# Rows gathered one by one from two issuing engines: five chunks on ScalarE, twenty on the sync engine

## The chip, the core and the metric

The kernel runs on one NeuronCore of a Trainium2 chip. The metric is the device time of one execution in microseconds. A core has a matrix engine (TensorE, PE in the profile; its weight loads are PEld), VectorE (DVE), ScalarE (ACT), GpSimd (POOL) and a sync engine (SP), each with its own queue of instructions that runs in order. DMAs are issued from the queues of SP, ACT and POOL and carried out by 16 DMA engines. Engines wait for each other through semaphores.

## The reference

```python
h = jnp.maximum(_layernorm(x, axis=-1), 0.0)          # x: (12500, 128) f32
msgs = h[src]                                         # src, dst: 200000 edges, sorted by dst
agg = jax.ops.segment_sum(msgs, dst, num_segments=12500)
deg = jax.ops.segment_sum(jnp.ones((200000,)), dst, num_segments=12500)
agg = agg / jnp.maximum(deg, 1.0)[:, None]
y = jax.nn.relu(agg @ Wg + h @ Ws + bg)               # 128 -> 128
y = jnp.tanh(y @ W1 + b1)                             # 128 -> 512
y = jnp.tanh(y @ W2 + b2)                             # 512 -> 512
return x + (y @ W3 + b3)                              # 512 -> 128
```

One layer of a graph network: each node's feature row is normalised, the rows of its neighbours are averaged, and a small network of three layers follows. The edges are sorted by destination.

## The kernel before

**Set-up.** The normalised rows h are written to a table in DRAM, `htab` (lines 221 to 239). The 200000 edges are cut into 1563 chunks of 128 edges.

**One chunk.** The 128 source rows of a chunk come into a tile of 128 x 128. DVE builds a one-hot matrix from the destinations of eight chunks at a time (`onehot`, line 364: a comparison at 372 and a column sum at 382 for the degrees), in four buffers `oh_bufs` that are used in turn. PE multiplies rows by one-hot matrix (`add`, line 422) and so adds the rows to the sums of a block of 512 nodes in PSUM. All matmuls are recorded at line 290, all transposes at line 293, all activations at line 322, all copies on ScalarE at line 325.

**Three ways for rows to arrive.**

- `gather` (line 301): an indirect DMA issued by POOL fetches the 128 rows of a chunk from `htab` with an index column. It is recorded at line 303 as `rows<-htab,scol`. 1465 chunks come so, in the order of the list `order`. The pool `rows_in` has `AHEAD` = 48 tiles, and the loop issues a gather once `nxt < behind + AHEAD`; on the chip a gather waits until PE has used the tile's former content.
- 80 chunks (`raw`) are gathered straight from x during the set-up, and normalised later.
- `row_loads` (line 327): 18 chunks, listed in `slow`, are fetched row by row by the sync engine: `place` holds the byte offsets of their rows; a register load (line 333) takes 32 of these to registers, and 32 DMAs of 512 bytes each, one row each, follow (line 341, recorded at 299). A chunk takes four such sets, 128 DMAs. The pool `rows_one` has four tiles, so that rows are loaded long before they are used.

**The list of slow chunks.** A chunk is put on the list after every `EACH` = 72 others:

```python
if n <= 0:
    slow.append(c)
    n = EACH
else:
    n -= 1
```

**The network.** When the sums of a block are complete, its layers are worked off in small parts between the chunks: `go_on` issues one part (at most a matmul or two, and the activation that follows) after every second chunk (lines 678 to 680). ScalarE's Relu, Tanh and bias additions are needed by PE's next parts. DVE scales the sums (`mT`, line 523) and adds x at the end (`o`, line 579); `ps_t` and `ps_b` have one PSUM buffer each. From chunk `QUICK` = 1376 on the parts are placed by estimated times.

**Order.** `tc.keep_in_program_order` fixes each engine's instructions in the order in which the Python loop writes them. A part of the row loads is written per step of the loop (line 655): `next(loading, 0)` issues `TOGETHER` = 4 row DMAs each time the count of gathered chunks behind the loop passes another 72 x 4 / 128 = 2.25. Also on the sync engine's queue: the own rows of a block (`hb`, line 476), x (`xb`, line 499), and the stores of the result (`sp_dma` in `store`, 12 chunks after the sum, `LATE`). DMAs of the sync engine and of ScalarE share eight semaphores, which the framework hands out in turn; a DMA that gets a semaphore waits until the DMA that had it before has landed.

Of the kernel before, what the change touches and what calls it, by code (L numbers as in the profile page):

```python
# [22 lines left out]
F32 = mybir.dt.float32  # L23
# [8 lines left out]
P = 128  # L32
# [5 lines left out]
NRAW = 10  # L38
RAW0 = 256
STEP = 40  # L40
AHEAD = 48
SLOW0 = 160
EACH = 72
TOGETHER = 4
LOADS = 32
LATE = 12
LEAD = 16
QUICK = 1376
# [11 lines left out]
def windowed(ctx, tc, x, src, dst, Wg, Ws, bg, W1, b1, W2, b2, W3, b3, out, flag):  # L60
    nc = tc.nc
    N, D = x.shape
# [18 lines left out]
    def raw(c):  # L81
        return RAW0 <= c < RAW1 and (c - RAW0) % STEP < GRP


    slow, n = [], 0
    for c in range(SLOW0, NCH - 12):
        if raw(c):
            continue
        if n <= 0:
            slow.append(c)  # L90
            n = EACH
        else:
            n -= 1


    def first(w, span=per):
# [8 lines left out]
    blocks, n = [], 0  # L105
# [10 lines left out]
    rows_one = ctx.enter_context(tc.tile_pool(name="rows_one", bufs=4))  # L116
    rows_in = ctx.enter_context(tc.tile_pool(name="rows_in", bufs=AHEAD))
    ps_c = ctx.enter_context(tc.tile_pool(name="ps_c", bufs=1, space=PSUM))
# [8 lines left out]
    for t, a in ((rsrc, src), (rdst, dst)):  # L127
        a = a[RAW0 * P : RAW1 * P].rearrange("(u e) -> u e", u=NRAW)[:, : GRP * P]
# [46 lines left out]
    def centre(pool, xt, k, stats, bufs=2):  # L175
        nc.vector.tensor_reduce(stats[:, 0], xt, AX.X, ALU.add)
        nc.vector.scalar_tensor_tensor(xt, spread(stats[:, 0], k), -1.0 / D, xt, op0=ALU.mult, op1=ALU.add)
        sq = pool.tile([P, k, D], F32, name=f"sq{k}", bufs=bufs)
        nc.scalar.activation(sq, xt, AF.Square)
        nc.vector.tensor_reduce(stats[:, 1], sq, AX.X, ALU.add)  # L180

    def factors(stats):
        nc.scalar.activation(stats[:, 1], stats[:, 1], AF.Sqrt, bias=eps, scale=1.0 / D)
        nc.vector.reciprocal(stats[:, 1], stats[:, 1])
# [4 lines left out]
    with tc.tile_pool(name="setup", bufs=1) as sp, tc.tile_pool(name="ln", bufs=2) as ln:  # L189
# [59 lines left out]
        for c0, w in WINDOWS[1:]:  # L249
            v = low[:, c0:]  # L250
# [44 lines left out]
    def flat(t):  # L295
        return t.rearrange("p a b -> p (a b)")

    def sp_dma(*a):
        tc.keep_in_program_order(nc.sync.dma_start(*a))  # L299

    def gather(c):
        r = rows_in.tile([P, D], F32, name="rows")
# [7 lines left out]
    ROWB = 4 * D  # L310
    hbytes = htab.rearrange("n d -> (n d)").bitcast(U8)
# [3 lines left out]
    place = const.tile([len(slow), P], I32, name="place")  # L315
# [8 lines left out]
        def copy(*a):  # L324
            tc.keep_in_program_order(nc.scalar.copy(*a))

    def row_loads():
        for i, c in enumerate(slow):
            r = rows_one.tile([P, D], F32, name="srows")
            rows_t[c] = r  # L330
            rb = r.bitcast(U8)
            for p0 in range(0, P, LOADS):
                loads, vs = nc.values_load_multi_w_load_instructions(
                    place[i : i + 1, p0 : p0 + LOADS], engines=[mybir.EngineType.SP], min_val=0,
                    max_val=(N - 1) * ROWB,
                    skip_runtime_bounds_check_because="src holds rows of x, as the indirect DMAs take it to",
                )
                for ld in loads:
                    tc.keep_in_program_order(ld)
                for p, v in enumerate(vs, p0):  # L340
                    sp_dma(rb[p : p + 1, :], hbytes[bass.ds(v, ROWB)].rearrange("(o b) -> o b", o=1))
                    if (p + 1) % TOGETHER == 0:
                        yield

    def raw_stats(i):
        return stats_raw[:, :, i * GRP : (i + 1) * GRP]

    def raw_scaled(i):
        h = raw_rows[i]
        scale(h, h, GRP, raw_stats(i))  # L350
        for j in range(GRP):
            rows_t[RAW0 + i * STEP + j] = h[:, j]
# [11 lines left out]
    def onehot(g):  # L364
        k = min(GRP, NCH - g * GRP)
        lo, w = window(g * GRP)
        is_raw = raw(g * GRP)
        oh = ed.tile([P, GRP, W_RAW], F32, name="ohr", bufs=2) if is_raw else oh_bufs[g % OHS]
        if not is_raw and w < oh_w[g % OHS]:
            nc.vector.memset(oh[:, :, w : oh_w[g % OHS]], 0.0)  # L370
            oh_w[g % OHS] = w
        nc.vector.tensor_tensor(  # L372
            oh[:, :k, :w], lane[:, None, :w].to_broadcast([P, k, w]),
            dloc[:, g * GRP : g * GRP + k][:, :, None].to_broadcast([P, k, w]), op=ALU.is_equal,
        )
        ohs[g] = oh
        step, n = (oh.shape[2], w) if is_raw else (PITCH - per, w + per * (k - 1))
        cnt = ed.tile([P, PITCH], BF16, name="cnt", bufs=16)
        part, row, col = oh.ap
        shifted = bass.AP(tensor=oh.tensor, offset=oh.offset, ap=[part, [col[0], n], [step * col[0], k]])  # L380
        with nc.allow_low_precision(reason="whole numbers up to the chunks of a group"):
            nc.vector.tensor_reduce(cnt[:, :n], shifted, AX.X, ALU.add)  # L382
        counts[g] = (lo, n, cnt)
# [10 lines left out]
    def count(b):  # L394

        n, m = blocks[b]
        dg = flat(ps_m.tile([P, 4, P], F32, name="pm"))
        groups = sorted({c // GRP for c in reach[b]})
        for g in groups:
            lo, w, cnt = counts[g]  # L400
            a0, a1 = max(lo, n), min(lo + w, n + m)
            pe.matmul(
                dg[:, a0 - n : a1 - n], ones, cnt[:, a0 - lo : a1 - lo], start=(g == groups[0]), stop=(g == groups[-1]),
                skip_group_check=True,
            )
        rd = ml.tile([P, BLK], F32, name="rd", bufs=3)
        nc.vector.tensor_scalar(rd[:, :m], dg[:, :m], 1.0, None, op0=ALU.max)  # L407
        nc.vector.tensor_reduce(total[:, b : b + 1], dg[:1, :m], AX.X, ALU.add)
        nc.vector.reciprocal(rd[:, :m], rd[:, :m])  # L409
        rds[b] = rd  # L410
# [189 lines left out]
        )  # L600

    order = [c for c in range(NCH) if not raw(c) and c not in slow]
    loading = row_loads()
    work, done, nxt, behind = [], 0, 0, 0
    ngrp = -(-NCH // GRP)
    span = BLK // per
# [2 lines left out]
    def store(upto):  # L609
        while stores and stores[0][0] <= upto:  # L610
            sp_dma(*stores.pop(0)[1:])

    def soonest():
        two = work[: 2 if len(work) > 1 and work[1][3] < work[0][3] and work[0][4] else 1]
        return min(two, key=lambda w: max(w[2], now), default=None)
# [16 lines left out]
    for c in range(NCH):  # L632
        g = c // GRP
        at = c
        store(c if c >= QUICK else c - LATE)
        if c % GRP == 0 and g + 2 < ngrp:
            onehot(g + 2)
            if raw((g + 2) * GRP):
                raw_scaled(((g + 2) * GRP - RAW0) // STEP)
            if 2 <= g < 2 + NRAW:  # L640
                centre(ed, raw_rows[g - 2], GRP, raw_stats(g - 2), bufs=1)
            if g == 2 + NRAW:
                factors(stats_raw)

        while c % GRP == GRP // 2 and counted < len(blocks) and reach[counted][-1] // GRP <= g + (c >= QUICK):
            count(counted)
            counted += 1
        while nxt < len(order) and nxt < behind + AHEAD:
            gather(order[nxt])
            nxt += 1  # L650
        if not raw(c) and c not in slow:
            behind += 1
            batch = behind * P // (EACH * TOGETHER)
            if behind > SLOW0 - 3 * EACH and batch > (behind - 1) * P // (EACH * TOGETHER):
                next(loading, 0)
        if c >= QUICK:

            there = 7.5 + 1.251 * (NRAW * GRP + order.index(c)) if c not in slow else 0
            while soonest() and max(now, soonest()[2]) < there:
                go_on(soonest())  # L660
            now = max(now, there) + 0.27
        add(c)

        lead = LEAD if c < QUICK else 2
        if done < len(blocks) and (c - lead if across[done] else c) >= reach[done][-1]:
            if across[done]:
                merge(done)
            quick = reach[done][-1] + LEAD >= QUICK

            before = done - 1 if done and reach[done - 1][-1] + LEAD < QUICK else None  # L670
            work.append([layers(done, before), 0, 0, 0, quick and blocks[done][1] <= P])
            done += 1

        if c % span == span - 10 and (c // span + 1) * BLK < N:
            own_turned(c // span + 1)
            if (c // span + 2) * BLK < N:
                own(c // span + 2)
        if c < QUICK:
            if c % 2 == 0:
                go_on(work[0] if work else None)  # L680
        if c == QUICK:
            for b, (_, n) in enumerate(blocks):
                if n < BLK:
                    own_part(b)
# [379 lines left out]
```

## Time and profile before

| | |
|---|---|
| median of 11 runs | 2327.13 us (2317.41 to 2333.45) |
| the profiled execution | 2333.16 us, its span 2331.2 us |
| granted TensorE clock, mean | 0.791 |
| PE busy | 1322.9 us (57%) |
| DVE busy | 1066.6 us (46%) |
| POOL busy | 1463.3 us (63%) |
| ACT busy | 227.2 us (10%) |
| gathers from `htab` on POOL | 1465, 945 ns each |
| one-row DMAs on the sync engine | 2304, from 117 to 2070 us |

The profile is of one execution. Busy time counts instructions that compute or, on POOL, make the descriptors of a gather; DMA-issuing instructions on SP and ACT do not count as busy (they stand under SPq and ACTq). "Idle before" is the time in which an engine stood still just before an instruction, followed by what ended it as far as the semaphores tell; "remote" is a releaser that the profile could not name, "issue" a wait for nothing that it shows. The set-up takes the first 110 us; POOL's first gather from `htab` starts at 111 us and the last ends at 2268 us.

### The profile page before, as it was taken

To read this page: it belongs to the slowest core of one execution; us is meant where nothing else is said; L and a number is where in the kernel's file an instruction comes from. 1 tells how busy PE (TensorE), PEld (TensorE's weight loads), DVE (VectorE), ACT (ScalarE), POOL (GpSimd) and SP (SyncE) were. 2 spreads that over 40 slices of the span, in tenths; PEclk is the share of its full clock that TensorE was granted. 3 is DMA by queue.
4 is the path that set the end of the run, shared out by engine and by line. 5 is a ranking of instruction groups with operands and counts; after the bars stand their busy time and mean duration, and the time that the engine had idled before them with its cause. 6 is when DMAs were issued, how large, how long until landed. Compare 5 with 4: busy or idle time off the path is not lost. (4 is left out here: it accounts for less than half of the span.)

```text
span 2331.2 us, 19720 instructions
## 1 busy us (share of the span) xinstructions
PE 1322.9 (57%) x5212; PEld 866.5 (37%) x5212; DVE 1066.6 (46%) x651; ACT 227.2 (10%) x362; POOL 1463.3 (63%) x1553
## 2 busy tenths in 40 slices
PE   0132345556766766765565665565655655654668
PEld 0022233334444444443343433343433433432437
DVE  5924283545446544643443453443534434533522
ACT  1100010001111011101000000000000000010013
POOL 7675656666666656666666666666666666646650
PEclk9998567788887877877787787777877887776879
DMA  6721111212222212212222222222222221221210
GB/s 166 217 53 39 51 46 51 55 51 60 61 54 56 59 51 55 60 51 55 52 61 55 51 60 55 52 57 55 54 58 55 55 55 51 60 54 45 64 46 9
DMA packets 124131, 139.34 MB, mean 60 GB/s; under 512 B 32776, under 2 KB 98454, under 8 KB 123816
## 3 DMA queue, kind: packets, MB, share of 16 engines
q0 software_dynamic: 49440, 101.35, 17.1%
q1 hardware_dynamic: 71374, 33.32, 5.2%
q10 hardware_dynamic: 3196, 3.32, 0.6%
q8 instruction: 43, 0.70, 0.1%
q14 instruction: 78, 0.64, 0.1%
HBM read 125.06 MB, written 12.82 MB: 59 GB/s over the span
## 5 line engine op out<-in xcount | busy, mean ns | idle before, releaser
L303 POOL DMA_INDIRECT rows<-htab,scol x1465 | 1384.8, 945 | 778.3 <-issue 338.9
L290 PE MATMUL pm<-h,w 128*128 128x512 f32 (+4 forms) x1344 | 716.1, 628 | 185.1 <-ACT h L322 113.3
L372 DVE TENSOR_TENSOR oh<-shared,dloc 128x1152 f32<-128x1152 f32 (+2 forms) x186 | 243.8, 1316 | 914.3 <-remote 370.6
L290 PEld LDWEIGHTS agg<-oh,rows 128*128 128x128 f32 x2098 | 387.5, 225 | 468.2 <-issue 418.2
L290 PE MATMUL agg<-oh,rows 128*128 128x144 f32 (+3 forms) x2098 | 435.1, 329 | 221.0 <-issue 179.7
L382 DVE TENSOR_REDUCE cnt<-oh 128x200 bf16<-128x1600 f32 (+2 forms) x186 | 525.0, 2827 | 4.8
L290 PEld LDWEIGHTS pm<-h,w 128*128 128x128 f32 x1344 | 242.6, 220 | 225.8 <-ACT h L322 122.3
L290 PEld LDWEIGHTS edge<-oh,rows 128*128 128x128 f32 x832 | 149.9, 216 | 145.9 <-issue 140.9
L290 PE MATMUL edge<-oh,rows 128*128 128x144 f32 (+2 forms) x832 | 160.4, 312 | 37.2 <-issue 34.5
L293 PE MATMUL pt<-ident,hb 128*128 128x128 f32 x98 | 26.1, 410 | 233.8 <-DVE o L579 184.4
L322 ACT ACTIVATE h<-pm,b2c 128x512 f32<-128x512 f32 (+4 forms) x112 | 70.9, 633 | 665.7 <-remote 244.9
L290 PE MATMUL pm<-mT,wg 128*128 128x512 f32 (+4 forms) x56 | 42.3, 848 | 122.2 <-DVE mT L523 106.7
L293 PEld LDWEIGHTS pt<-ident,hb 128*128 128x128 f32 x98 | 16.5, 206 | 241.3 <-DVE o L579 189.5
L322 ACT ACTIVATE h<-pm,b1c 128x512 f32<-128x512 f32 (+4 forms) x112 | 69.1, 632 | 265.9 <-remote 183.2
L146 POOL DMA_INDIRECT raw<-in_x_dram,rsrc x80 | 77.6, 970 | 25.6 <-issue 24.1
L290 PE MATMUL pm<-cnt,ones 128*128 128x200 bf16 (+7 forms) x294 | 38.7, 233 | 84.0 <-issue 83.8
L409 DVE RECIPROCAL rd<-rd 128x512 f32<-128x512 f32 (+4 forms) x28 | 81.8, 2920 | 0.0
L407 DVE TENSOR_SCALAR rd<-pm 128x512 f32<-128x512 f32 (+4 forms) x28 | 17.3, 620 | 115.7 <-remote 75.4
L290 PEld LDWEIGHTS <-ones 128*128 128x128 bf16 x294 | 23.8, 101 | 95.5 <-issue 94.8
L290 PEld LDWEIGHTS pm<-mT,wg 128*128 128x128 f32 x56 | 11.4, 254 | 127.2 <-DVE mT L523 110.8
L322 ACT ACTIVATE h<-pm,bgc 128x512 f32<-128x512 f32 (+4 forms) x28 | 17.7, 632 | 356.4 <-PE agg L290 159.1
L205 PE MATMUL pm<-ident,idx_f 98*128 98x98 f32 x32 | 6.2, 376 | 75.8 <-issue 75.8
(68 smaller groups left out, 496.4 us busy)
## 6 DMA issues: line engine op xcount, KB each, us to landing
srows<-htab SPq DMA_DIRECT2D x2304, 0.5 KB
rows<-htab,scol POOLq DMA_INDIRECT x1465
hb<-htab SPq DMA_DIRECT2D x24, 256.0 KB
xb<-in_x_dram SPq DMA_DIRECT2D x23, 256.0 KB
out_dram<-o SPq DMA_DIRECT2D x23, 256.0 KB
htab<-h SPq DMA_DIRECT2D x6, 896.0 KB
xt<-in_x_dram SPq DMA_DIRECT2D x5, 896.0 KB
raw<-in_x_dram,rsrc POOLq DMA_INDIRECT x80
```

Source lines behind the costliest of these rows:

```text
L146: nc.gpsimd.indirect_dma_start(out=t[:, j, :], out_offset=None, in_=x, in_offset=bass.IndirectOffsetOnAxis(ap=rsrc[:, g, j : j + 1], axis=0),)
L205: nc.tensor.transpose(p[:, q, :NROW], rf[:, (q0 + q) * P : (q0 + q + 1) * P], ident[:NROW, :NROW])
L290: tc.keep_in_program_order(nc.tensor.matmul(*a, **k))
L293: tc.keep_in_program_order(nc.tensor.transpose(*a, **k))
L303: nc.gpsimd.indirect_dma_start(out=r, out_offset=None, in_=htab, in_offset=bass.IndirectOffsetOnAxis(ap=scol[:, c : c + 1], axis=0),)
L322: tc.keep_in_program_order(nc.scalar.activation(*a, **k))
L372: nc.vector.tensor_tensor(oh[:, :k, :w], lane[:, None, :w].to_broadcast([P, k, w]), dloc[:, g * GRP : g * GRP + k][:, :, None].to_broadcas ...
L382: nc.vector.tensor_reduce(cnt[:, :n], shifted, AX.X, ALU.add)
L407: nc.vector.tensor_scalar(rd[:, :m], dg[:, :m], 1.0, None, op0=ALU.max)
L409: nc.vector.reciprocal(rd[:, :m], rd[:, :m])
```

## The change

Two lists take the place of one: `slow_s` for the sync engine (after every 66 others) and `slow_a` for ScalarE (after every 200 others, in the range below `QUICK`). With these constants the lists hold 20 and 5 chunks; before there were 18. So POOL gathers 1458 chunks where it gathered 1465. ScalarE gets the same kind of row loads, through `act.dma`, with register loads of its own, and a batch of four is written when the count of gathered chunks passes another 200 x 4 / 128 = 6.25, from the 49th on. The new tiles `arows` (four, in the pool `rows_one`) take the room of four of the tiles for gathers: `AHEAD` is 44 instead of 48. `in_turn` links each DMA of the two queues to the DMA written before it, whichever queue that was on, without a wait on the chip: it keeps the scheduler from handing out the eight semaphores in another order than that of the program.

```diff
-AHEAD = 48
+AHEAD = 44
 SLOW0 = 160
-EACH = 72
+EACH = 66
+EACH_A = 200
 TOGETHER = 4
...
-    slow, n = [], 0
+    slow_s, slow_a = [], []
+    ns, na = 0, 2 * EACH
     for c in range(SLOW0, NCH - 12):
         if raw(c):
             continue
-        if n <= 0:
-            slow.append(c)
-            n = EACH
+        if ns <= 0:
+            slow_s.append(c)
+            ns = EACH
+        elif na <= 0 and c < QUICK:
+            slow_a.append(c)
+            na = EACH_A
         else:
-            n -= 1
+            ns -= 1
+            na -= 1
+    slow = slow_s + slow_a
...
+    turn = []
+
+    def in_turn(start):
+
+        tc.keep_in_program_order(start)
+        if turn:
+            tc.add_manual_dep(
+                start.ins, turn.pop(),
+                mybir.DependencyInfo(mybir.DependencyClass.NoSync, mybir.DependencyReason.DATA), reason="in_turn",
+            )
+        turn.append(start.ins.name)
+
     def sp_dma(*a):
-        tc.keep_in_program_order(nc.sync.dma_start(*a))
+        in_turn(nc.sync.dma_start(*a))
...
+        def dma(*a):
+            in_turn(nc.scalar.dma_start(*a))
+
-    def row_loads():
-        for i, c in enumerate(slow):
-            r = rows_one.tile([P, D], F32, name="srows")
+    def row_loads(chunks, engine, dma, name, together):
+        for c in chunks:
+            i = slow.index(c)
+            r = rows_one.tile([P, D], F32, name=name)
...
-                    place[i : i + 1, p0 : p0 + LOADS], engines=[mybir.EngineType.SP], min_val=0,
+                    place[i : i + 1, p0 : p0 + LOADS], engines=[engine], min_val=0, max_val=(N - 1) * ROWB,
...
-                    sp_dma(rb[p : p + 1, :], hbytes[bass.ds(v, ROWB)].rearrange("(o b) -> o b", o=1))
-                    if (p + 1) % TOGETHER == 0:
+                    dma(rb[p : p + 1, :], hbytes[bass.ds(v, ROWB)].rearrange("(o b) -> o b", o=1))
+                    if (p + 1) % together == 0:
                         yield
...
-    loading = row_loads()
+    loading = row_loads(slow_s, mybir.EngineType.SP, sp_dma, "srows", TOGETHER)
+    loading_a = row_loads(slow_a, mybir.EngineType.Activation, act.dma, "arows", TOGETHER)
...
             batch = behind * P // (EACH * TOGETHER)
             if behind > SLOW0 - 3 * EACH and batch > (behind - 1) * P // (EACH * TOGETHER):
                 next(loading, 0)
+            batch = behind * P // (EACH_A * TOGETHER)
+            if behind > 48 and batch > (behind - 1) * P // (EACH_A * TOGETHER):
+                next(loading_a, 0)
```

More of the change, by code (lines that the diff above doesn't have):

```diff
@@ L333, in row_loads @@
                 loads, vs = nc.values_load_multi_w_load_instructions(
-                    place[i : i + 1, p0 : p0 + LOADS], engines=[mybir.EngineType.SP], min_val=0,
-                    max_val=(N - 1) * ROWB,
+                    place[i : i + 1, p0 : p0 + LOADS], engines=[engine], min_val=0, max_val=(N - 1) * ROWB,
                     skip_runtime_bounds_check_because="src holds rows of x, as the indirect DMAs take it to",
```

## The prediction

> **What bounds the kernel now.** I began with the page: which engine is busy, and which group has the most time.
>
> ```profile
> PE 1322.9 (57%) x5212; PEld 866.5 (37%) x5212; DVE 1066.6 (46%) x651; ACT 227.2 (10%) x362; POOL 1463.3 (63%) x1553
> ...
> L303 POOL DMA_INDIRECT rows<-htab,scol x1465 | 1384.8, 945 | 778.3 <-issue 338.9
> ```
>
> No engine is full. The largest group is the 1465 gathers on POOL, 945 ns each. The next view is the POOL timeline around 1410 us (start, duration, line, idle time before), which shows their rhythm:
>
> ```profile
> 1407.14 0.94 POOL L303 DMA_INDIRECT rows<-htab,scol  x1 [0.31 <-issue]
> 1408.39 0.95 POOL L303 DMA_INDIRECT rows<-htab,scol  x1 [0.30 <-issue]
> 1409.67 0.95 POOL L303 DMA_INDIRECT rows<-htab,scol  x1 [0.33 <-remote]
> 1413.92 0.95 POOL L303 DMA_INDIRECT rows<-htab,scol  x1 [3.30 <-remote]
> 1415.17 0.95 POOL L303 DMA_INDIRECT rows<-htab,scol  x1 [0.30 <-issue]
> ```
>
> A free gather takes 1.25 us from start to start; after some 13 of them POOL stands still for about 3 us. The windows view says how much that is: 70 gathers start between 1400 and 1500 us, so 1.43 us each, and the ten hundreds from 900 to 1900 hold 69 to 71. The POOL rows of the waits view name the releasers (total us, times, longest):
>
> ```profile
> POOL rows L303 <- remote: 188.0, 138, 5.4
> POOL rows L303 <- PE agg L290: 136.8, 143, 18.2
> POOL rows L303 <- PE edge L290: 63.1, 48, 8.9
> ```
>
> A gather waits for PE to have used the chunk 48 places back, and counted against the chunks that PE has released, POOL does stand 45 to 50 gathers ahead from 300 us on. So the gather stream always runs into the end of its buffers. The time adds up accordingly: 1465 x 1.25 = 1831 us of gathers, about 325 us of POOL idle time beyond the usual 0.30 us between two, some 111 us before the first gather, and 63 us from the last to the end: together the span of 2331 us.
>
> Why is PE late? Three timelines at the same moment, PE, ACT and DVE:
>
> ```profile
> 1413.68 2.08 PE L290 MATMUL pm<-h,w 128*128 128x512 f32 x2 [6.11 <-ACT h L322]
> 1412.94 0.69 ACT L322 ACTIVATE h<-pm,bgc 128x512 f32<-128x512 f32 x1 [21.26 <-remote]
> 1413.68 1.36 DVE L372 TENSOR_TENSOR oh<-shared,dloc 128x1152 f32<-128x1152 f32 x1 [14.14 <-remote]
> ```
>
> PE waits for ScalarE's Relu, and ScalarE had been idle for 21 us. Following its wait in the program, it needs a matmul that the record ends at 1398.9 us: the hop from PE to ScalarE took 14 us. Over the stretch 400 to 2050 us such hops lose 3 to 5 us at the median where the waiter was idle; after the last gather they lose 0.04 us. So while POOL streams, PE, ScalarE and DVE hand work over slowly, POOL runs out of buffers, and in its pause they catch up. The chain through ScalarE counts although ACT is 10% busy.
>
> **The change, part by part.** Sums are made against the profiled execution, 2333.16 us (span 2331.2); it lies 6.0 us above the median of the runs, 2327.13, and I take those 6 us off at the end.
>
> *Gathers removed.* By the lists in the code, the sync engine loads 20 chunks (18 before) and ScalarE 5, so POOL has 7 gathers fewer: 7 x 1.25 = 8.8 us off POOL's stream, which is additive as shown. The bounds are 0 (the pauses grow by as much) and 7 x 1.43 = 10.0 us (each takes its share of the pauses along). I take 8.8.
>
> *44 instead of 48 buffers.* While POOL is always at its limit, the depth only shifts it against PE. It costs at the end: POOL issues its last gather with PE four chunks further on. Those four chunks pass at 1.43 us instead of the 0.245 us that PE shows when it runs free (8 pieces, four chunks, in 0.98 us at 1417.39): 4 x 1.19 = 4.7 us, between 0 and 5.7. Nothing starves: rows land 2 to 3 us after the issue, and 44 gathers are 55 us.
>
> *More row loads on the sync engine.* 256 more of them, 2560 in all. Each one is off the path, since its rows are wanted some 130 chunks later. What counts is how long the sync engine takes; its timeline, and the first row of its own waits (total us, times, longest):
>
> ```profile
> 1395.24 44.50 SPq L299 DMA_DIRECT2D srows<-htab  x50
> ```
>
> ```profile
> SPq L299 <- DVE o L579: 193.7, 10, 102.1
> ```
>
> 50 loads in 44.5 us are 0.89 us each; 2304 in the 1953 us from 117 to 2070 are 0.85; less the 232 us in which it waited for DVE (193.7, 24.4, 7.6 and 6.3 us in that view) they are 0.75. So the queue had about 12% of slack, and 11% more loads use it up. By itself that costs nothing.
>
> *Row loads on ScalarE.* 640 of them in 160 batches of four, and 20 register loads. They stand in program order between the activations, on the engine that PE waits for. The nearest rows are ScalarE's own one-row DMAs of the setup and the sync engine's register loads (tile views, ns min/median/max):
>
> ```profile
> L314 ACTq DMA_DIRECT2D at_i<-in_src_dram x18: 229/263/700, 32.6 to 69.5; - x18
> ```
>
> ```profile
> L333 SPq TENSOR_LOAD <-place x72: 16/1396/2600, 115.8 to 2044.2; - x72
> ```
>
> With a 29 ns register move, one load costs 0.29 us by that row, and 0.89 us by the sync engine's row in the stage where the loads now stand. I laid the batches at their places in the new program over the idle times that ScalarE has there in the old trace. They fall into 138 gaps, median 6.5 us, so most are hidden; 23 gaps are under 2 us. With 1.4 us for a register load, what does not fit adds up to 16 us at 0.29, 37 us at 0.5 and 99 us at 0.89. The short gaps are those after a flush, when issues are quick, so I take 0.5; and as PE has other ready chunks behind part of these hops, half of it reaches the end: 18 us. Bounds 0 and 99.
>
> *Semaphores shared in program order.* Eight DMA semaphores go round over both queues. A load on ScalarE now waits until the load eight places earlier, one of the sync engine's, has landed, and the sync engine's loads behind a batch wait for ScalarE's. Before, the sync engine ran up to 100 chunks ahead; now both go in step. Behind the waiting load on ScalarE stands the next activation, behind that PE, and behind PE POOL's buffers. One round is 200 x 4 / 128 = 6.25 gathered chunks, 8.9 us at 1.43 us each. In it the sync engine has 12.1 loads: 9.05 us at 0.75, 10.8 us at 0.89. So ScalarE is held by 0.1 to 1.9 us a round, 160 rounds: 20 to 300 us; 0 if POOL's longer pauses speed the sync engine up (after the pause at 1436 us its issues are 0.25 to 0.4 us apart). I take 20 us: the wait-free price, since stores are late less often when both go in step.
>
> Sum: -8.8 + 4.7 + 18 + 20 = +34 us, 2367 on the profiled execution, 2361 on the median.
>
> One rule speaks against the step itself. Row: a row load costs the sync engine 0.85 us of issue. The Trainium skill, "DMA: Bandwidth & Descriptors", section "Issuing engines are not separate DMA queues", says that DMAs from several engines run on the same 16 DMA engines and that a second issuer only saves issue time, usually small. By the rule 640 loads would buy 640 x 0.85 = 544 us of the sync engine's time, none of it on the path, and the sum would be the seven gathers less the buffers, about -4 us; by the rows the issue time is not small, and it lands on the engine that PE waits for.
>
> **The rivals.** *Faster:* ScalarE's loads all fit into its idle time and the sync engine keeps step. For it: gaps of 6.5 us against 1.2 us a batch at 0.29, ACT 10% busy. Against it: the 23 short gaps. Then only the gathers count: 8.8 to 10 us off, up to 4.7 back, and some luck in the pauses: 2315 to 2322 us. *Lockstep decides:* the sync engine needs 10 us or more a round while ScalarE comes by every 8.9. For it: 0.85 to 0.89 us per load measured. Its price is 1.1 us and more x 160, over 175 us, less what POOL's longer pauses give back: 2430 to 2600 us; it decides from 0.83 us per load on (12.1 x 0.83 = 10.0). *Nothing to measure:* gain and cost cancel within 0.2% (4.7 us, about what a measurement of this kernel can tell): 2322 to 2332.
>
> **How the numbers follow.** My forecast, a loss of some tens of us (2335 to 2430), has 0.49; the lockstep 0.17; faster 0.27; no difference 0.07. The likeliest is 2361 us. The range runs from the faster case's lower end, 2314, to 2450, which leaves out most of the lockstep case. Faster by over 0.2%: 0.27, within: 0.07, slower: 0.66, as 0.49 + 0.17.
>
> **What would show it.** Right: POOL has 1458 gathers, and the hundreds between 400 and 1600 us hold 67 to 69 gathers instead of 70; ScalarE's waits view names the DMA of srows as a releaser; PE's waits for ScalarE's h (113.3 us in 28 times now) grow; from 1700 us on, where ScalarE has no more loads, the pace is as before. Lockstep: the sync engine's loads come in even groups of twelve with waits on arows, and POOL's idle time grows by over 150 us. Wrong: the same 70 gathers per 100 us and an end 5 to 10 us earlier, or ScalarE's loads hidden and the loss elsewhere, in the last 270 us for instance.

## The result and the profile after

The changed kernel takes 2395.45 us, median of 12 runs (2381.25 to 2407.3); the kernel before, in the same sets, 2325.64 us. The ratio is 1.030 (95% interval 1.029 to 1.032): **slower by 3.0%**. The profiled execution of after took 2384.07 us (span 2382.3), that of before 2333.16 (span 2331.2), so the profiles show 51 of the 70 us.

The experiments below were run in four sets, each with the kernel before beside it, and the kernel before took 2327 us in some sets and 1954 us in others, with the same program. The same chip showed both (1953.89 us in the first set, 2327.37 in the third), so it is not the chip; what it is, no run here tells. I call them the **2327 condition** and the **1954 condition**. The result above and the prediction belong to the first.

The page of after, busy time of the engines and the largest group:

```profile
PE 1321.6 (55%) x5212; PEld 876.6 (37%) x5212; DVE 1068.1 (45%) x651; ACT 225.2 (9%) x362; POOL 1456.4 (61%) x1546
...
L322 POOL DMA_INDIRECT rows<-htab,scol x1458 | 1378.1, 945 | 841.6 <-issue 343.2
```

The work is the same; POOL has 7 gathers fewer and 63 us more idle time before gathers (778.3 in the page of before). The windows view counts the gathers between 400 and 1600 us (span, busy time, number). First before, then after:

```profile
400.00:1600.00 1200.00, 778.44 (x825) 0.79 0.21 55
```

```profile
400.00:1600.00 1200.00, 752.14 (x797) 0.77 0.21 54
```

That is 68.8 and 66.4 per 100 us (the view counts gathers that touch the stretch). The waits view of after says on whom POOL waits, and what ScalarE's activations stand behind (us, times, longest); the last line is from the sync engine's own waits:

```profile
POOL rows L322 <- PE agg L297: 204.8, 144, 39.4
...
ACT h L341 <- DMA arows<-htab: 408.3, 47, 26.3
...
ACT h L341 <- DMA srows<-htab: 164.1, 16, 37.0
```

```profile
SPq L318 <- DMA arows<-htab: 83.2, 13, 55.6
```

The second line is new: an activation comes late because a row load stands ahead of it. The third names a load of the *sync engine* as what ScalarE waited for. The first has one wait of 39.4 us. Here it is in the timelines of POOL, PE, ACT and SP (start, duration, what, idle before):

```profile
358.25 0.95 POOL L322 DMA_INDIRECT rows<-htab,scol  x1 [39.42 <-PE agg L297]
```

```profile
355.42 2.08 PE L297 MATMUL pm<-h,w 128*128 128x512 f32 x2 [40.87 <-ACT h L341]
```

```profile
308.11 1.49 ACTq L347 DMA_DIRECT2D arows<-htab  x4
...
328.19 26.44 ACTq L347 DMA_DIRECT2D arows<-htab  x24
354.68 0.69 ACT L341 ACTIVATE h<-pm,bgc 128x512 f32<-128x512 f32 x1 [26.26 <-DMA arows<-htab]
```

```profile
229.99 80.96 SPq L318 DMA_DIRECT2D srows<-htab  x30
311.29 0.17 SPq L318 DMA_DIRECT2D hb<-htab  x1
311.56 39.14 SPq L318 DMA_DIRECT2D srows<-htab  x68
```

Read it from the bottom. The sync engine issues only 30 loads between 230 and 311 us, and none from 253 to 309: its next one wants a semaphore whose last user is ScalarE's first batch, and that batch stands in ScalarE's queue behind a square (part of normalising the raw chunks) that starts only at 305.7 us (the wait of 55.6 us above). In before ScalarE comes to its squares as late, and the sync engine, which waits for no load of ScalarE, issues some 126 loads between 202 and 306 us. After the stop the sync engine makes up for it, 0.58 us a load; meanwhile 24 loads of ScalarE wait one by one for the sync engine's, 26 us. Behind them stands the first Relu, behind that PE (40.9 us), behind PE POOL's buffers (39.4 us).

Where the 51 us of the two profiles are, from the starts of the gathers (a pause is what exceeds 1.25 us from start to start):

| us | before | after | difference |
|---|---|---|---|
| first gather from htab | 110.9 | 107.3 | -3.6 |
| steps between gathers x 1.25 | 1830.0 | 1821.3 | -8.8 |
| pauses, gathers 1 to 150 | 43.2 | 74.9 | +31.7 |
| pauses, 150 to 300 | 29.1 | 35.4 | +6.3 |
| pauses, 300 to 1100 | 165.6 | 205.3 | +39.7 |
| pauses, 1100 to the last | 88.0 | 78.9 | -9.0 |
| last gather to the end | 64.3 | 59.1 | -5.2 |

ScalarE's last load is issued at 1789 us, at about gather 1100: behind it the pauses are no longer than before.

How much did ScalarE wait for the semaphores? I took, for each of its 640 row loads, the time from the end of the register move in front of it to its start, and looked up in the program whose load had the semaphore. All 640 follow a DMA of the sync engine (628 of them a row load), and together they stood 957 us; half of them start less than 1.3 us after that DMA's issue, so ScalarE goes at the sync engine's pace. The other way round it is 169 us. The 160 batches themselves take 2.14 us each, 0.54 us a load. So of the time that the loads take in ScalarE's queue most is waiting: 957 us, against some 170 us for issuing 640 loads (0.27 us each with the register move) and 44 us for 20 register loads. How much of either reaches the end this does not say.

### The profile page after: what moved, and what is told of

The parts are those of the page before. It is cut to its first block, busy times and chain, and to the rows that moved or that the text cites. A ratio compares the mean times of both kernels' runs of the same rounds, so it can differ in the third digit from the quotient of the medians.

```text
span 2382.3 us, 21546 instructions
## 1 busy us (share of the span) xinstructions
PE 1321.6 (55%) x5212; PEld 876.6 (37%) x5212; DVE 1068.1 (45%) x651; ACT 225.2 (9%) x362; POOL 1456.4 (61%) x1546
## 5 line engine op out<-in xcount | busy, mean ns | idle before, releaser
L297 PE MATMUL pm<-h,w 128*128 128x512 f32 (+4 forms) x1344 | 726.3, 637 | 334.7 <-issue 136.4
L297 PEld LDWEIGHTS agg<-oh,rows 128*128 128x128 f32 x2080 | 395.9, 233 | 415.9 <-issue 372.3
L297 PE MATMUL agg<-oh,rows 128*128 128x144 f32 (+4 forms) x2080 | 437.7, 336 | 160.4 <-issue 118.2
L297 PE MATMUL pm<-cnt,ones 128*128 128x200 bf16 (+7 forms) x294 | 32.8, 251 | 82.7 <-issue 70.4
L601 DVE TENSOR_TENSOR o<-pt,xb 128x512 f32<-128x512 f32 x23 | 15.8, 687 | 76.4 <-remote 68.7
```

The source lines that it names most:

```text
L297: tc.keep_in_program_order(nc.tensor.matmul(*a, **k))
L601: nc.vector.tensor_tensor(o[:, :whole], po[:, :whole], xb[:, :whole], op=ALU.add)
```

## The experiments

**Theory A:** the two queues hold each other through the shared semaphores, most of all at the start. **B:** ScalarE's own issue time. **C:** 11% more loads overfill the sync engine. **D:** 44 buffers are too few. E and F are formed on the way. The edits are against the changed kernel where nothing else is said.

### First set: before 1953.89 us

`late_start`:

```diff
-            if behind > 48 and batch > (behind - 1) * P // (EACH_A * TOGETHER):
+            if behind > 88 and batch > (behind - 1) * P // (EACH_A * TOGETHER):
```

> ScalarE's row loads start with the first step after the 88th gathered chunk instead of the 48th, which puts the first batch behind the last of the ten squares; all five chunks, all 640 loads and the shared semaphores stay. Theory A (the two queues lock each other through the shared semaphores, and most of the loss is one lock at the start, POOL's 39.4 us pause at 305 to 345 us): the stretch 300 to 400 us holds 65 gathers or more instead of 41, and the time falls by 30 to 42 us, to 2353 to 2365 us. Theory B (the time that ScalarE needs to issue 640 loads, on PE's path): as many loads in nearly the same gaps, so under 10 us less: 2385 to 2400 us.

`no_act_rows`:

```diff
+    slow_a = []
     slow = slow_s + slow_a
```

> The change without ScalarE: the five chunks come by POOL's gathers (1463 of them), the sync engine keeps its 20, 44 buffers. Theory A and B (the loss is ScalarE's part): pace as before, 69 to 71 gathers per 100 us between 500 and 1600 us, 2 gathers fewer than before (-2.5 us) and 0 to +5.7 us for the buffers: 2323 to 2329 us. Theory C (the sync engine's 11% more loads use up its slack): 67 or 68 gathers per 100 us stay, 2345 us or more. Theory D (44 buffers are too few): the same 67 or 68 per 100 us, 2340 us or more.

`act_rows_alone`:

```diff
+    slow_s = []
     slow = slow_s + slow_a
```

> ScalarE loads its five chunks, 640 loads at the same places, the sync engine loads none (its 20 chunks come by gathers: 1478), so that ScalarE's loads wait nearly always for ScalarE's own. Theory A: pace of the kernel before, 69 to 71 gathers per 100 us from 500 to 1600 us, no long pause at 305 us; 13 gathers more than before, +16 us, and 0 to +5.7 us for the buffers: 2342 to 2349 us, and 5 to 8 us less than the kernel without any row loads. Theory B: 67 or 68 gathers per 100 us, some 30 us more: 2370 to 2390 us, and 20 us or more above the kernel without any row loads.

`no_rows`:

```diff
+    slow_s, slow_a = [], []
     slow = slow_s + slow_a
```

With no list left, this run also keeps one unused row of offsets in `place`, so that the tile is not empty.

> No row loads at all: 1483 gathers, 18 more than before (+22.5 us), 0 to +5.7 us for 44 buffers: 2349 to 2356 us if the row loads cost the rest nothing, in every theory; less, down to 2327 us, if the sync engine's loads of the kernel before slow the other engines' hand-overs.

| | us | ratio, 95% interval | gathers |
|---|---|---|---|
| late_start | 1945.42 | 0.9955 (0.9938 to 0.9972) | 1458 |
| no_act_rows | 1951.54 | 0.9985 (0.9975 to 0.9994) | 1463 |
| act_rows_alone | 1969.34 | 1.0084 (1.0064 to 1.0103) | 1478 |
| no_rows | 1977.38 | 1.0117 (1.0100 to 1.0134) | 1483 |

None of the expected times came: the set met the 1954 condition, which I had not known of. In it POOL never pauses: 80 gathers in every 100 us, and the time is, within 2 us, a straight line in the number of gathers: from 1458 to 1483 31.96 us, 1.28 us each. Beyond that neither ScalarE's 640 loads nor the sync engine's 2560 cost anything here. Of the theories this decides only that none of the costs is there in *every* condition. The first expectation has the long pause of after at 305 to 345 us; by the timeline above it lies from 319 to 358 us.

### Second set: before 1953.63 us

`after_again` is the changed kernel, `late_again` the first kernel of the set above. First after_again:

> The changed kernel as it is, beside the kernel before on the chip that these runs get. In the last four runs the kernel before took 1954 us instead of 2327, at a granted clock of 0.905 instead of 0.791, and POOL never waited for a buffer. Theory E (what the change costs depends on the hand-overs between PE and the other engines: where they take 3 to 5 us, ScalarE's row loads lengthen POOL's waits; where they are quick, only the number of gathers counts): on a chip with quick hand-overs 7 gathers fewer give -8.7 us, ratio 0.995 to 0.997, with one pause of POOL at the start of ScalarE's loads at the most; on a chip with the slow ones a ratio of 1.03 again. Theory A in its strict form (the lock of the two queues costs time wherever it runs): a ratio of 1.01 or more on every chip, with a pause of POOL of 20 us or more when ScalarE's loads begin.

Then late_again:

> The changed kernel with ScalarE's loads from the 88th gathered chunk on instead of the 48th. Theory E with quick hand-overs: 0 to 3 us from the changed kernel. On a chip where the kernel before takes about 2327 us: theory A 30 to 42 us less than the changed kernel, theory B (ScalarE's issue time) under 10 us less.

`sync_all_25`, against before:

```diff
-EACH = 72
+EACH = 53
```

> The kernel before with a chunk on the sync engine after every 53 others: 25 chunks, 3200 loads, no loads on ScalarE, 48 buffers, 1458 gathers as in the changed kernel. With quick hand-overs one load takes the sync engine 0.37 us, so 3200 take 1190 us of some 1650: all fit, and the time is that of the changed kernel or up to 2 us less (ratio 0.994 to 0.996). On a chip where a load takes 0.75 to 0.85 us, 3200 take 2400 us and more, and PE waits for rows of the sync engine: slower than the kernel before by 50 us or more; if the sync engine's pace rises while PE waits, by less.

Again the 1954 condition. after_again 1945.85 us, ratio 0.9961 (0.9947 to 0.9975); late_again 1945.39, 0.9963 (0.9950 to 0.9975); sync_all_25 1945.54, 0.9958 (0.9942 to 0.9975). So **the change makes the kernel 0.4% faster here**, by its 7 gathers (8.75 us at 1.25), and who issues the row loads makes no difference. The Trainium skill, "DMA: Bandwidth & Descriptors", section "Issuing engines are not separate DMA queues", says that a second issuing engine saves only issue time; 1945.85 us with two issuers and 1945.54 with one agree with it.

But the hold is there all the same. ACT's timeline and waits of after_again, then POOL's waits:

```profile
246.68 27.04 ACTq L347 DMA_DIRECT2D arows<-htab  x24
273.77 0.69 ACT L341 ACTIVATE h<-pm,bgc 128x512 f32<-128x512 f32 x1 [26.86 <-DMA arows<-htab]
```

```profile
ACT h L341 <- DMA arows<-htab: 47.8, 7, 26.9
```

```profile
POOL rows L322 <- PE agg L297: 32.6, 107, 0.3
```

ScalarE is held for 27 us at the same place of the program, and PE behind it, yet POOL's longest wait is 0.3 us, the usual step between two gathers. In this trace PE's largest waits are for the rows themselves (285.7 us in 417 waits for agg, 0.7 us at the median), so it goes close behind POOL, and most of the 44 tiles must still be free when the hold comes: in 27 us POOL issues 22 gathers. Nor is the sync engine the slow one: ScalarE's loads stood 184 us for the sync engine's, the sync engine's 411 us for ScalarE's. Theory A in its strict form falls. Theory E takes its place, in a new form: a hold of ScalarE costs what POOL's buffers cannot absorb.

### Third set: before 2327.37 us

To test E, the same kernels with 8 tiles for gathers, on before (48 there), after and late_start; and a kernel with more rows on both queues (late_start with `EACH = 44`, `EACH_A = 130`: 29 and 8 chunks).

```diff
-AHEAD = 44
+AHEAD = 8
```

`before_8_buffers`:

> The kernel before with 8 tiles for gathers instead of 48, as the reference for the next two runs. Theory E (ScalarE's loads cost what POOL cannot absorb with its buffers): with few buffers POOL is at their limit on every chip, as it was in the profiled run of before with 48. On a chip with quick hand-overs PE waits for rows most of the time, so it is only a few chunks behind POOL: pauses in the stages where PE is held for over 10 us, 20 to 100 us in all.

`after_8_buffers`:

> The changed kernel with 8 tiles for gathers instead of 44, to be set against the kernel before with 8. With 44 buffers on a chip with quick hand-overs ScalarE was held for 26.9 us at 246 us by its first loads, and POOL did not notice. Theory E: with 8 buffers, 10 us of gathers, POOL stands still for some 17 us there and for some 6 us at 329 us, and the change loses 10 to 30 us against the kernel before with 8, although it has 7 gathers fewer. Theory F (the holds of ScalarE are harmless wherever PE has other ready work): it gains 5 to 9 us against the kernel before with 8, as with many buffers.

`late_8_buffers`:

> As the one above, with ScalarE's loads from the 88th gathered chunk on. Theory A (the largest single cost is the first batch, written ahead of ScalarE's last squares): 15 us or more less than with the start at the 48th. Theory B (the holds are spread evenly over the 160 batches): within 5 us of it.

`more_rows`:

> More chunks row by row: one on the sync engine after every 44 others (29 chunks), one on ScalarE after every 130 (8 chunks), from the 88th on, 44 buffers; 1446 gathers, 19 fewer than before. With quick hand-overs: 19 x 1.25 = 24 us less than the kernel before (1930 us where that takes 1954), if the sync engine keeps step: 3712 loads at 0.37 us are 1373 us of some 1650. Where hand-overs take 3 to 5 us: slower than the kernel before by 100 us or more, since 3712 loads at 0.75 us need 2784 us.

This set met the 2327 condition.

| | us | ratio, 95% interval |
|---|---|---|
| before_8_buffers | 2295.87 | 0.9859 (0.9839 to 0.9879) |
| after_8_buffers | 2371.97 | 1.0193 (1.0164 to 1.0222) |
| late_8_buffers | 2356.44 | 1.0121 (1.0104 to 1.0138) |
| more_rows | 2711.53 | 1.1661 (1.1638 to 1.1685) |

*The change with 8 tiles* costs 76 us, with 48 and 44 it was 70. So in this condition the number of tiles hardly matters for it (D falls as the cause), and F falls. E's 10 to 30 us missed: they had been worked out from holds under quick hand-overs. For slow ones E had named a ratio of 1.03, and 2371.97 / 2295.87 is 1.033, but that 1.03 was the recorded result carried over, so it is no test of E.

*The start* is worth 15.5 us. POOL's timeline at the lock, first after_8_buffers, then late_8_buffers:

```profile
306.97 0.94 POOL L322 DMA_INDIRECT rows<-htab,scol  x1 [38.78 <-PE agg L297]
```

```profile
285.62 0.94 POOL L322 DMA_INDIRECT rows<-htab,scol  x1 [16.76 <-PE agg L297]
```

The pause falls from 38.8 to 16.8 us, as theory A has it, and B (within 5 us) does not fit; the two intervals in the table do not meet. Not all is kept: before_8_buffers has a pause of 10.1 us there, and late_8_buffers has more pauses later (227 us in gathers 300 to 1100, against 211 in after_8_buffers). The 15.5 us are those of the medians; the profiled execution of late_8_buffers, 2369.14 us, was the slowest of its runs. And they are a fifth of the loss: late_8_buffers still takes 60.6 us more than before_8_buffers. So theory A's other half, that the start is *most* of the loss, falls with 8 tiles; with 44 the late start was not run in this condition.

*more_rows* had been expected to lose 100 us or more, and loses 384. Its waits:

```profile
ACT h L341 <- DMA arows<-htab: 945.8, 97, 30.6
ACT h L341 <- DMA srows<-htab: 271.9, 22, 24.2
```

ScalarE's 1024 loads stand 1481 us for the sync engine's, and POOL makes 55 gathers per 100 us. The sync engine issues up to 176 DMAs in 100 us, 0.57 us each, where it had issued 115 to 146 in before and after between 500 and 1600 us. So the 0.75 us of the prediction was no fixed limit of the sync engine; where POOL pauses more, it goes faster. Nor does PE wait for late rows: neither in after nor in more_rows does its list of waits name srows or arows (in late_8_buffers it does, 33.5 us in three waits). Theory C in its plain form, the sync engine too late with its chunks, does not fit that.

*before_8_buffers* was a surprise: 1.4% faster than before, with an unchanged pace between 400 and 1600 us:

```profile
400.00:1600.00 1200.00, 777.91 (x825) 0.84 0.20 55
```

The last gather starts at 2271 us instead of 2267, and the end comes 28 us later instead of 64: with 48 tiles PE has up to 48 chunks to work off behind the last gather, with 8 at most 8. Before the end the waits only change places: PE's waits for gathered rows (agg) are 355.0 us with 8 tiles and 12.1 us with 48.

### Fourth set: before 1954.0 us

`act_alone_8_buffers` is act_rows_alone with 8 tiles, to tell A from B in the 2327 condition.

> ScalarE's 640 loads at the same places, none on the sync engine (its 20 chunks come by gathers: 1478), 8 tiles for gathers. In the trace of the changed kernel ScalarE's loads stood 957 us in all for a load of the sync engine that had the semaphore before; here they wait for ScalarE's own loads of two batches earlier. Where hand-overs take 3 to 5 us (the kernel before near 2327 us, with 8 buffers 2296): theory A (the waits for the sync engine's loads cost the time): those waits fall below 50 us, the stretches from 400 to 1600 us hold 68 to 70 gathers, and 13 gathers more than before give 2296 + 16 = 2312 us, a ratio of 0.99 to 1.00. Theory B (ScalarE's issue time costs it): 64 to 67 gathers per 100 us, and 2345 us or more, a ratio over 1.008. Where hand-overs are quick (the kernel before near 1954 us): the 1969 us of the same kernel with 44 tiles if 8 are enough there, up to 1990 us if PE is ever held for over 10 us.

It met the 1954 condition, so A and B could not be told apart by it. There it took 2000.82 us (1.0232, 1.0215 to 1.0249), 31.5 us more than with 44 tiles. POOL's waits show why:

```profile
POOL rows L323 <- PE agg L298: 92.3, 215, 14.7
```

PE is held for over 10 us now and then even when hand-overs are quick, and 8 tiles cover 10 us. POOL's pauses are 28 us in this trace and 0 with 44 tiles: here theory E's new form shows itself. Few tiles are better in one condition and worse in the other. No version is shown to beat both kernels in both conditions: before_8_buffers does at 2327 us, where alone it ran; at 1954 us after_again, late_again and sync_all_25 are equally ahead, and the last two were not run at 2327 us.

## Why the prediction was right or wrong

**The forecast** (a loss of some tens of us, 2361 in 2335 to 2430) held for the recorded time. Its terms did not all hold, and the loss was seen in the 2327 condition alone. That the recorded runs met this condition was luck: in the other the rival "faster" would have come true.

- *Gathers, -8.8:* right, in both conditions: POOL's step is 1.25 us in every trace, and without pauses the line over four kernels gives 1.28 us per gather. The 70 gathers that the prediction has starting between 1400 and 1500 us are those that touch the hundred; 69 start in it.
- *Buffers, +4.7:* wrong sign. The step that failed is that POOL's last gather would come at the same place of PE's work and the rest would pass slowly. In after the stretch behind the last gather is 5.2 us shorter; 40 tiles fewer made the kernel 31.5 us faster, 0.8 us per tile.
- *More loads on the sync engine, 0 by itself:* true in the 1954 condition (no_act_rows, 2.35 us faster with 2 gathers fewer). In the 2327 condition it was not run by itself; that the sync engine issues more per 100 us in more_rows, and that PE never waits for its rows in after, speak against a full queue.
- *ScalarE's issue, +18:* the price of a load, taken as 0.5 us, was 0.54 including the waits within a batch, and 0.27 without any wait; a register load took 2.26 us at the median, not 1.4. What it costs the end is not separated from the next term. In the 1954 condition it is nothing.
- *Semaphores, +20:* the mechanism was right, the size too small and the place missed. I had priced even holds of 0.1 to 1.9 us a round. Measured are 957 us, 6 us a round, of which POOL's pauses show 31.7 + 6.3 + 39.7 = 78 us with ScalarE's issue in it, against the 38 of both terms; and 32 of them lie ahead of gather 150, in one chain: batches written behind the squares, which I never laid against the sync engine's queue. I had laid ScalarE's batches over its idle times only from the side of ScalarE.
- *The sum:* +34 predicted, +51 in the profiles, +70 between the medians. The step "6 us off at the end" assumed that after's profile would lie above its median like before's; it lies 11 us below. So the +34 was half of the loss, with the two large terms together too small and the buffers on the wrong side.

The signs came as written: 1458 gathers; ScalarE's waits name srows; PE's waits for h grew from 113.3 to 135.0 us, by one long wait rather than by many; the pace from 1700 us on is the old one. The hundreds held 66.4 gathers, a little under the 67 to 69. Of the lockstep rival the waits on arows are there (83.2 us), the growth of POOL's idle time by 150 us is not (63).

The rule weighed in the prediction would have given -4 us. In the 1954 condition that is near the truth (-7.8 us); in the 2327 condition the second issuer costs time, through what it issues or through what it is coupled to.

**Open:** what makes the 2327 condition; how the 40 us between gathers 300 and 1100 (and the 60.6 us that the late start leaves with 8 tiles) divide between ScalarE's issue time, its waits for the sync engine and the 256 loads more on the sync engine, since the runs meant for it met the other condition; and why fewer tiles leave the pace as it is. That the waits decide is argued from their 957 us, not shown by a run.

## What to carry to other kernels

Before you give DMAs to a second engine, find out whether the two queues share semaphores in program order: then the first DMA of the one can stop the other for as long as the one is busy elsewhere, and afterwards the catching up holds both. Lay the new instructions over the queue that they are coupled to, not only over the idle time of their own engine, and start them behind the last long wait of that engine (15.5 us of 76 here). Measure in every condition that the machine shows: the same edit was +3.0% and -0.4% here, and 8 tiles instead of 48 helped in the one and, in a like kernel, 8 instead of 44 hurt in the other.

## What the runs showed of the hardware

- The same kernel on the same chip took 1954 us in one set and 2327 in another. Gathers take the same 944 and 945 ns; PE is busy for 1321.6 us in after (2327 condition) and 1365.5 us in after_again (1954), so it is not computing that takes longer, though the granted clock is lower; what differs is the waiting. In the 1954 condition POOL's wait between gathers is never over 0.3 us with 44 tiles or more, and PE waits 46 us for h in after_again against 135 in after. The granted clock is 0.90 to 0.92 against 0.78 to 0.79 in before and after, and 0.76 to 0.84 in the profiles of the third set.
- The sync engine's own instructions are uneven in the 2327 condition. These are the register moves in front of its 2560 row loads in after, then in no_act_rows (1954 condition), in ns, shortest, median and longest:

```profile
L318 SPq MOVE srows<-htab x2560: 2/29/1402, 111.7 to 2214.9; - x197
```

```profile
L319 SPq MOVE srows<-htab x2560: 29/29/29, 99.4 to 1744.6; - x197
```

In after a fifth of them take over 300 ns, mostly about 700; ScalarE's 640 moves in the same trace all take 29 ns. Whether this is a cause or a sign of the condition, no run tells.

- Traces of the 2327 condition must be read with care: that of after holds 10574 semaphore updates, that of after_again, the same program, 36614, so more releasers are missing or guessed. And 53 of ScalarE's 640 loads in after start up to 1.7 us *ahead* of the record of the DMA that they wait for, so the sync engine's records come late there.
- A row load costs its queue 0.37 us on the sync engine in the 1954 condition (48 in 17.81 us in the timeline of no_act_rows), 0.57 to 0.89 in the 2327 condition. The DMA instruction itself takes 228 ns at the median in both, but in after a fifth of the sync engine's take over 300 ns.
- A register load of 32 values took 2.1 to 2.3 us at the median in after on either engine (in before, 1.4 us by the sync engine's records).
